# Cross-attention and ternary feed-forward on one core: the second normalisation's factors from one inverse root each, the output bias as a product of 128 rows, and new figures for the planner

## The chip, the cores and the metric

The kernel runs on one core of a Trainium2 chip. The core has a matrix engine (PE, TensorE; its weight loads are listed apart as PEld), a vector engine (DVE), a scalar engine (ACT), a general engine (POOL, GpSimd) and a queue engine (SP) that issues transfers; 16 DMA engines carry these out. The metric is device microseconds of one execution. The kernel before takes 1246.66 us (median of 3 runs, 1245.68 to 1249.71). A measurement of this kernel can tell a difference of about 0.3% from none.

## The reference

One decoder-like block on x of 4 x 2048 x 512 (float32), with a context of 4 x 77 x 512 and a mask over the 77 keys.

```python
def _layernorm(x, eps=1e-5):
    return (x - mean(x)) / sqrt(var(x) + eps)

# cross-attention, 16 heads of 32
Q = norm(x) @ Wq.T + bq;  K = ctx @ Wk.T + bk;  V = ctx @ Wv.T + bv
probs = softmax(where(mask == 0, -inf, Q K^T / sqrt(32)))
x = x + (probs V) @ Wo.T + bo

# feed-forward with quantised rows and ternary weights, hidden size 2048
act_quant(x):  s = 127 / clip(max|x| per row, 1e-5);  round(x * s) / s
weight_quant(w):  s = 1 / mean|w|;  clip(round(w * s), -1, 1) / s
h = act_quant(norm(x)) @ weight_quant(w1).T
h = silu(depthwise_conv1d(h, conv_w (3 taps), conv_b))     # along the sequence
x = x + act_quant(h) @ weight_quant(w2).T
```

A masked key takes the mean of the kept keys in the kernel and adds nothing to the sums. The quantity that the change is about is the second normalisation with the row's quantisation behind it: for each row of x after attention the mean, the variance, the largest |x - mean|, and from them the factor by which the row is multiplied before rounding and the factor that undoes it later (`dq`).

## The kernel before, in words

The 8192 rows are 64 blocks of 128 rows (`plan_block`, t = 0 to 63). Attention goes block by block; the query products go over pairs of blocks (`plan_queries`); the feed-forward goes over tiles of up to four blocks (`plan_hidden`, `TILES = [2, 2, 4, ..., 4, 3, 1]`, 18 tiles).

A block t passes these steps, each a `Step` with an engine, a cost in ns, a due time and the tiles that it uses and makes:

- First normalisation (`plan_norm`): ACT sums and squares (L714, L715), DVE scales the variance (L728), POOL takes the power -1/2 (L737) and applies it (L745). The result is split into two half-precision halves: the high half (`xn_hi`, ACT or POOL, L765 or L767, due at `O["hi"]`) and the low half (`xn_lo`, POOL, L795, due at `O["lo"]`). SP transposes both (`xn_transpose`, L800, due at `O["xT"]`).
- Query product of the pair on PE (L1067 to L1069, three products for the halves), bias on ACT or DVE (L1077, L1079).
- Scores in four groups of four heads on PE (L820), row maxima on DVE (L825), exponentials on ACT (L832). Due at `O["sc"]` and `O["sc_step"]` times the group.
- Probabilities in two halves of eight heads: split into high and low (L765 or L767, and L857 on POOL; due at `O["ph0"]`, `O["ph1"]`), transposed by SP (L861), multiplied by the values on PE (L869), divided by their sums on DVE (L881, L886).
- Context: split (L765 or L767, L918), transposed (L922), multiplied by the output weights on PE (`product`, L929 to L934). The first of its 13 matmuls, L929, is the output bias: three bfloat16 rows that add up to it (`bo3`, 3 x 512), multiplied by three rows of ones (`ones_bf`, 3 x 128).
- Residual on DVE (`residual`, L944): the product times a constant plus x, which SP has loaded a second time (`load_again`, L938, due at `O["xb"]` from the product), with the row's sum from the accumulator. L947 turns the sum into the negative mean. SP stores the block (L951) for the end.
- Second normalisation: `squares` on ACT (L970: (x - mean)^2 with their sum), `largest` on DVE (L977 the row's maximum of the squares, L978 variance plus eps), `roots` on POOL (L982: power 0.5 of the maximum and -0.5 of the variance in one operation), `scales` on DVE (L989 to L992, four operations on one number per row, each but one made from the one before), `quantise` on POOL (L997: add, multiply, to float16 with an offset of the exponent that rounds). SP transposes it (L1005); PE spreads `dq` over the columns (L689) and ACT copies it (L1013).

A tile of the feed-forward then goes through 16 groups of 128 hidden channels: product on PE (L1105), times `dq` on DVE (L1119), middle tap on ACT (L1130), the two other taps by the letter in `conv`: `b` both on DVE (L1145), `c` the first on DVE and the second on ACT and POOL (L1152, L1159), `d` both on ACT and POOL. Then SiLU on ACT (L1205), maxima on DVE (L1210), transposed maxima (L1241, L1246), scales on DVE (L1251 to L1256), spread and copied (L689, L1263), rounding on POOL (L1284), the second product on PE (L1304), the residual on DVE (L1314) and the store (L1320).

Which engine does a step that can go to two is set by `WHO`, one row for each stretch of blocks that `PARTS` bounds. Nothing at run time chooses: `Plan.schedule` walks through all steps in a modelled time, gives each engine the ready step with the earliest due time (in blocks, `t` plus an offset of the table `O`), takes the cost from the figure in `add`, and so writes one fixed order for each engine. The chip keeps that order and waits where a step's inputs or buffers are late. The buffers that bear on the change are `xb` (3), `xT` (2) and `qT` (8).

The two weights of the feed-forward are made ternary ahead (`plan_ternary`): `scale` (L644 to L649) takes the mean of |w|, from it the factor `deq` and its inverse.

Of the kernel before, what the change touches and what calls it, by code (L numbers as in the profile page):

```python
# [24 lines left out]
P = 128  # L25
# [52 lines left out]
PARTS = (12, 44, 56)  # L78
# [51 lines left out]
class Plan:  # L130
# [3 lines left out]

    LAT, SWITCH = {"PE": 197, "DVE": 130, "ACT": 130, "Pool": 75}, 1283
# [95 lines left out]
def xattn_bitffn_kernel(  # L231
# [123 lines left out]
    add("SP", 2500, -29, [], {"B": "y"}, load_ctx, lat=2300)  # L355
# [123 lines left out]
    add("DVE", 1700, -20, ["B"], {"kept": None}, kept_keys)  # L479
    for oc in range(EC):  # L480
# [4 lines left out]
            "DVE", 2000, pr, ["A", "B", ("kT", oc), "kept", ("s", "wq")], {("km", oc): None},  # L485
# [60 lines left out]
    for g in range(CG):  # L546
# [3 lines left out]
            "DVE", 1700, pr, [("pv", g), "kept"] + [("vm", g - 1)] * (g > 0),  # L550
# [37 lines left out]
    bo3 = fixed([3, E], BF16, "bo3")  # L588
# [15 lines left out]
    add("DVE", 3000, -11, [("s", "v"), ("s", "wo")], {"bos": None}, output_bias, lock=True)  # L604
    add("SP", 1800, -10, ["bos"], {"bo3": None}, gather_bias, lat=2300)
# [7 lines left out]
    def plan_ternary(dst, src, deq, name, prio):  # L613
# [28 lines left out]
        def scale():  # L642
# [20 lines left out]
        for i in range(2):  # L663
# [3 lines left out]
            for k in (2 * i, 2 * i + 1):  # L667
                eng = "ACT" if name in SUM_ACT else "DVE"
                add(eng, 2202, pr, [w], {(name, k, "t"): None}, partial(total, k))
        add(  # L670
            "DVE", 600, prio + 1.2, [(name, i, "t") for i in range(4)],
# [106 lines left out]
    def plan_block(t):  # L778
# [27 lines left out]
        add("SP", 400, early, [], {x: "x"}, load, lat=2500)  # L806
# [133 lines left out]
        def residual():  # L940
# [6 lines left out]
            nc.vector.tensor_scalar(o["rs"][:, 0:1], o["rs"][:, 0:1], -1.0 / E, None, ALU.mult)  # L947
# [15 lines left out]
        add("DVE", 800, t0 + 0.17, [xb, ("po", t), ("pod", t)], {("x1", t): None}, residual)  # L963
        add("SP", 350, t0 + 0.2, [xb, ("x1", t)], {("x1d", t): None}, keep, lat=2100)

        def squares():
# [4 lines left out]
                o["xm"], o["xb"], AF.Square, bias=r[:, 0:1], accum_out=r[:, 2:3]  # L971
            )

        def largest():

            r = o["rs"]
            nc.vector.tensor_reduce(r[:, 1:2], o["xm"], AX.X, ALU.max)  # L977
            nc.vector.tensor_scalar(r[:, 2:3], r[:, 2:3], 1.0 / E, EPS, ALU.mult, ALU.add)  # L978

        def roots():  # L980
            r = o["rs"][:, 1:3]
            nc.gpsimd.tensor_tensor(r, r, roots_of, ALU.pow)  # L982

        def scales():

            r = o["rs"]
            root, rstd = r[:, 1:2], r[:, 2:3]
            o["dq"] = small.tile([P, 1], F32, tag="dq1", name=f"dq_{t}")
            nc.vector.tensor_scalar(root, root, rstd, 1e-5, ALU.mult, ALU.max)  # L989
            nc.vector.tensor_scalar(o["dq"], root, deq1, None, ALU.mult)  # L990
# [411 lines left out]
```

## Time and profile before

| | us |
|---|---|
| median of 3 runs | 1246.66 (1245.68 to 1249.71) |
| the profiled execution, its own time | 1247.53 |
| its span, first to last instruction | 1245.7 |
| mean granted clock of TensorE | 0.968 |
| first bias product L929 starts / last | 97.8 / 1114.5 |
| first / last scales L989 | 115.6 / 1134.8 |
| TENSOR_REDUCE L977, mean | 0.671 |
| POOL power L982, mean | 0.707 |
| quantise L997, mean | 0.770 |

All times are of one execution. An engine's busy time is the union of its instructions. A row of the order of time gives the start, the duration, the engine, the line, and the operation with its operands; instructions of a pipelined engine overlap, so that the distance between starts, not the duration, is what one costs. In the list of waits the engine on the left stood idle until the instruction on the right was done; "issue" is idle time for which the profile shows no cause.

### The profile page before, as it was taken

What the parts mean: (1) busy time and instruction counts of PE and PEld (TensorE: products, weight loads), DVE (VectorE), ACT (ScalarE), POOL (GpSimd) and SP (SyncE); (2) the same over time, 40 slices, a digit from 0 to 9 for tenths busy, and PEclk for the clock granted to TensorE, in tenths of its full rate; (3) what the DMA queues carried; (4) which work ended last, traced back from release to release, by engine and by line L of the source; (5) the groups of instructions that cost most, each with busy time, mean ns of one, the idle gap of its engine ahead of it and who ended that gap; (6) DMA issues with size and microseconds to landing.
All of it is one profiled execution on the core that took longest, in us unless ns stands there. A gap on an engine that the chain in (4) does not pass through costs nothing. (4 is left out here: it accounts for less than half of the span.)

```text
span 1245.7 us, 24178 instructions
## 1 busy us (share of the span) xinstructions
PE 1122.5 (90%) x8191; PEld 732.2 (59%) x8191; DVE 1046.1 (84%) x2271; ACT 1016.0 (82%) x2345; POOL 982.8 (79%) x922
## 2 busy tenths in 40 slices
PE   4668889999899999999999999999999999986776
PEld 2345556666666666666666666666666665654332
DVE  5766488889899988988899989989998989998773
ACT  3666799989899888988989898989898988765651
POOL 3378767786897979697888879697979898778665
PEclk9869899999999999999999999999999999998987
DMA  7687967877676666667676767758576766541211
GB/s 246 250 183 158 186 126 137 175 172 151 133 154 160 140 156 155 157 149 168 136 161 144 190 145 165 154 145 179 132 166 163 166 127 160 121 111 47 68 60 58
DMA packets 403203, 185.45 MB, mean 149 GB/s; under 512 B 356307, under 2 KB 356947, under 8 KB 402568
## 3 DMA queue, kind: packets, MB, share of 16 engines
q1 hardware_dynamic: 402005, 183.62, 64.2%
q8 instruction: 64, 1.05, 0.4%
q14 instruction: 59, 0.48, 0.1%
q10 hardware_dynamic: 1075, 0.30, 0.1%
HBM read 65.13 MB, written 34.84 MB: 80 GB/s over the span
## 5 line engine op out<-in xcount | busy, mean ns | idle before, releaser
L1284 POOL TENSOR_TENSOR gq<-y,qsb 128x1024 f16<-128x1024 f32 (+3 forms) x144 | 309.6, 2167 | 11.9 <-PE pf L1304 10.6
L1105 PE MATMUL ph<-xqT,w1q 128*128 128x257 f16 (+3 forms) x2048 | 277.8, 277 | 18.1 <-DVE h L1119 17.3
L1304 PE MATMUL pf<-w2q,gq 128*128 128x512 fp8e4 x1024 | 265.7, 387 | 14.2 <-DVE xr L1314 7.7
L832 ACT ACTIVATE pr<-psc,nmx 128x77 f32<-128x77 f32 x1024 | 248.4, 337 | 27.7 <-DVE nmx L825 25.2
L1130 ACT ACTIVATE py<-h,cb_sb,cw_sb 128x512 f32<-128x512 f32 (+3 forms) x279 | 208.3, 747 | 68.2 <-DVE y L1145 67.8
L1105 PEld LDWEIGHTS <-w1q 128*128 128x128 fp8e4 x2048 | 198.5, 99 | 88.1 <-issue 38.4
L1119 DVE TENSOR_TENSOR h<-ph,dqb 128x514 f32<-128x514 f32 (+3 forms) x288 | 180.3, 626 | 39.9 <-PE ph L1105 37.8
L857 POOL TENSOR_TENSOR ph<-pr,ph 128x616 f16<-128x616 f32 x128 | 174.3, 1363 | 37.2 <-ACT ph L765 35.6
L820 PE MATMUL psc<-kblk,qT 128*128 128x308 f32 x512 | 184.1, 448 | 16.5 <-ACT pr L832 14.0
L1145 DVE SCALAR_TENSOR_TENSOR y<-h,cw_sb,py 128x512 f32<-128x512 f32 (+3 forms) x279 | 190.1, 681 | 10.4 <-POOL gq L1284 5.8
L1304 PEld LDWEIGHTS <-gq 128*128 128x128 f16 x1024 | 99.1, 99 | 108.8 <-issue 22.9
L1159 POOL TENSOR_TENSOR y<-y,ta 128x512 f32<-128x512 f32 (+3 forms) x100 | 114.2, 1142 | 54.9 <-ACT ta L1152 29.0
L1210 DVE TENSOR_REDUCE mx<-y 128x256 f32<-128x2048 f32 (+2 forms) x66 | 145.6, 2209 | 12.4 <-ACT y L1205 12.1
L1067 PE MATMUL pq<-xT,wq_hi 128*128 128x256 f16 x512 | 142.6, 279 | 12.8 <-DMA xT<-hl 6.4
L1069 PE MATMUL pq<-xT,wq_lo 128*128 128x256 f16 x512 | 142.5, 278 | 0.0
L1068 PE MATMUL pq<-xT,wq_hi 128*128 128x256 f16 x512 | 142.5, 278 | 0.0
L1145 DVE SCALAR_TENSOR_TENSOR py<-h,cw_sb,py 128x512 f32<-128x512 f32 (+3 forms) x197 | 135.7, 689 | 8.0 <-ACT py L1130 7.0
L825 DVE TENSOR_REDUCE nmx<-psc 128x4 f32<-128x308 f32 x256 | 118.5, 466 | 26.7 <-PE psc L820 26.1
L1205 ACT ACTIVATE y<-y 128x2048 f32<-128x2048 f32 (+3 forms) x72 | 120.1, 1712 | 1.6 <-POOL y L1159 1.2
L820 PEld LDWEIGHTS psc<-kblk,qT 128*128 128x128 f32 x512 | 87.7, 196 | 44.2 <-ACT pr L832 26.0
L869 PEld LDWEIGHTS <-prT 128*128 128x128 f16 (+1 forms) x1920 | 87.9, 98 | 43.6 <-DMA prT<-ph 24.2
L869 PE MATMUL pa<-vblk,prT 128*128 128x66 f16 (+2 forms) x1920 | 93.5, 201 | 18.2 <-DMA prT<-ph 12.6
(156 smaller groups left out, 2043.2 us busy)
## 6 DMA issues: line engine op xcount, KB each, us to landing
x<-in_x SPq DMA_DIRECT2D x64, 256.0 KB
xb<-in_x SPq DMA_DIRECT2D x64, 256.0 KB
x<-xb SPq DMA_DIRECT2D x64, 256.0 KB
xr<-x SPq DMA_DIRECT2D x64, 256.0 KB
out<-xr SPq DMA_DIRECT2D x64, 256.0 KB
w<-in_w1T SPq DMA_DIRECT2D x2, 2048.0 KB
w<-in_w2T SPq DMA_DIRECT2D x2, 2048.0 KB
prT<-ph SPq DMA_TRANSPOSE x128
```

The costliest lines, as they stand in the source:

```text
L820: nc.tensor.matmul(psc, pair[p]["q", c][:, half], kb[:, c], start=True, stop=True)
L832: nc.scalar.activation(o["pr", c // 2][:, n : n + NK], o["psc", c][:, h], AF.Exp, bias=o["nmx", c][:, h : h + 1],)
L857: nc.gpsimd.tensor_tensor(ph[:, 1, :HR], o["pr", hf], ph[:, 0, :HR], ALU.subtract)
L869: nc.tensor.matmul(pa[:, h0:h1], prT[:n, l + j], v[:, r], start=(j == 0 and i == 0), stop=(j == NS - 1 and i == 2), skip_group_check=True,)
L1067: nc.tensor.matmul(pq, hi[:, ic, os], xs[:, 0, ic], start=first, stop=False)
L1105: nc.tensor.matmul(ph[:, i, :WH], w1q[:, c, f * P : (f + 1) * P], xqT[:, c, c0 : c0 + WH], start=(c == 0), stop=(c == EC - 1),)
L1119: nc.vector.tensor_tensor(in_parts(s["h", f]), s["ph", f][:, :parts, :WH], in_parts(tile_a[a]["dqb"]), ALU.mult,)
L1130: nc.scalar.activation(dst, s["h", f][:, 1 : 1 + T], AF.Identity, bias=cb_sb[:, f : f + 1], scale=cw_sb[:, f, 1:2],)
L1145: nc.vector.scalar_tensor_tensor(ins[dst](), s["h", f][:, i : i + T], cw_sb[:, f, i : i + 1], ins[src](), ALU.mult, ALU.add,)
L1210: nc.vector.tensor_reduce(s["m", g][:, c0:c1], ys[g][:, :, c0:c1].rearrange("p c t i -> p t c i"), AX.XY, ALU.max, apply_absolute_value=True,)
L1284: engine.tensor_tensor(gq[u][:, :, :T], y, q, ALU.mult)
L1304: nc.tensor.matmul(s["po", k], gq[f // 2][:, f % 2, k * P : (k + 1) * P], w2q[:, f], start=(f == 0), stop=(f == HC - 1),)
```

## The change

- The residual keeps the plain row sum (L947 goes). `squares` takes 512 times the difference, (sum - 512 x)^2, by a factor in the activation; the constants behind it take the powers of 512 back.
- `largest` makes the variance first, then the maximum, then a third operation that raises the maximum to a floor that follows the variance.
- `roots` takes the power -0.5 of both numbers, into a tile of its own.
- `scales` makes three numbers with one operation each: a factor and an offset for `quantise` and `dq`. The factor of the first weight (`deq1`) is no longer in `dq`: it is multiplied into the tap weights `cw_sb` once, in `scale`. The dependency of `scales` on the mean of the first weight goes.
- `quantise` multiplies first and then adds.
- In the hidden tile's scales the multiplication L1254 goes; the copy on ACT becomes an activation with that factor.
- `ones_bf` is 128 x 128 and `bo3` 128 x 512, cleared, with the bias in its first three rows.
- The planner: new due times `O`, other engines for some steps (`WHO`, `PARTS`), new costs, and all PE costs times 1.04.

The diff, with what only changes a cost figure partly left out:

```diff
@@ -61,10 +61,10 @@
 O = {
-    "load": -4.06, "sa": -2.75, "na": -2.65, "hi": -4.58, "lo": -3.66, "xT": -2.53, "q": -1.68,
-    "q_step": 0.51, "sc": -0.43, "sc_step": 0.24, "ph0": 0.1, "ph1": 0.49, "v0": 0.1, "v1": -2.09,
-    "cx": 1.28, "o": 2.9, "n": 3.9, "xq": 3.51, "xb": -1.09, "h": 5.09, "s": 1.03, "p8": 0.63,
-    "p8_step": 0.33, "f": 2.33,
+    "load": -4.04, "sa": -2.75, "na": -2.68, "hi": -4.88, "lo": -2.65, "xT": -4.55, "q": -1.66,
+    "q_step": 0.51, "sc": -0.43, "sc_step": 0.0, "ph0": 0.09, "ph1": 1.04, "v0": 0.1, "v1": -2.17,
+    "cx": 1.28, "o": 2.94, "n": 3.71, "xq": 3.39, "xb": -1.77, "h": 5.09, "s": 1.03, "p8": 0.7,
+    "p8_step": 0.3, "f": 2.1,
 }
 SILU_ALL = False
 COUPLE = False
@@ -75,15 +75,15 @@
-PARTS = (12, 44, 56)
+PARTS = (12, 44, 54)
 WHO = [
     {"sa": "A", "sf": "D", "xh": "A", "ch": "A", "ph": "AA", "q": "AAAA",
      "conv": "ccbbbbbbbbbbbcbb", "round": "PPPPPPPP"},
     {"sa": "A", "sf": "D", "xh": "P", "ch": "A", "ph": "AA", "q": "AAAA",
      "conv": "cccbbbcbbbbbbcbb", "round": "PPPPPPPP"},
-    {"sa": "A", "sf": "D", "xh": "A", "ch": "P", "ph": "AA", "q": "DAAA",
-     "conv": "cccbbbcbbbbbbcbb", "round": "PPPPPPPP"},
-    {"sa": "A", "sf": "D", "xh": "A", "ch": "P", "ph": "AP", "q": "AAAA",
+    {"sa": "A", "sf": "D", "xh": "A", "ch": "P", "ph": "AA", "q": "AAAA",
+     "conv": "cccbcbcbbbbbccbb", "round": "PPPPPPPP"},
+    {"sa": "A", "sf": "D", "xh": "A", "ch": "A", "ph": "AP", "q": "AAAA",
      "conv": "dccbbdcbbbbbdccb", "round": "PPPPPPPP"},
 ]
@@ -132,12 +132,14 @@
...
+    PACE = {"PE": 1.04}
...
+        cost *= self.PACE.get(eng, 1.0)
...
@@ -282,10 +284,7 @@
...
-    roots_of = fixed([P, 2], F32, "roots_of")
-    nc.gpsimd.memset(roots_of[:, 0:1], 0.5)
-    nc.gpsimd.memset(roots_of[:, 1:2], -0.5)
-    ones_bf = fixed([3, P], BF16, "ones_bf")
+    ones_bf = fixed([P, P], BF16, "ones_bf")
...
@@ -476,13 +475,13 @@
...
-    add("DVE", 1700, -20, ["B"], {"kept": None}, kept_keys)
+    add("DVE", 1880, -20, ["B"], {"kept": None}, kept_keys)
...
-            "DVE", 2000, pr, ["A", "B", ("kT", oc), "kept", ("s", "wq")], {("km", oc): None},
+            "DVE", 2530, pr, ["A", "B", ("kT", oc), "kept", ("s", "wq")], {("km", oc): None},
...
@@ -585,7 +584,8 @@
...
-    bo3 = fixed([3, E], BF16, "bo3")
+    bo3 = fixed([P, E], BF16, "bo3")
+    nc.gpsimd.memset(bo3, 0.0)
...
@@ -601,8 +601,8 @@
...
-    add("DVE", 3000, -11, [("s", "v"), ("s", "wo")], {"bos": None}, output_bias, lock=True)
-    add("SP", 1800, -10, ["bos"], {"bo3": None}, gather_bias, lat=2300)
+    add("DVE", 4330, -11, [("s", "v"), ("s", "wo")], {"bos": None}, output_bias, lock=True)
+    add("SP", 2430, -10, ["bos"], {"bo3": None}, gather_bias, lat=2300)
...
@@ -645,8 +645,11 @@
             pt = new([P, E], F32, "m", f"pt_{name}")
             nc.tensor.matmul(pt[:, 0:1], ones, tot, start=True, stop=True)
             nc.vector.tensor_scalar(mean, pt[:, 0:1], 1.0 / (HID * E), 1e-5, ALU.mult, ALU.max)
-            nc.vector.tensor_scalar(deq, mean, 1.0 / 127.0, 1.0 / QUANTUM, ALU.mult, ALU.mult)
+            q = QUANTUM * E if name == "w1" else QUANTUM
+            nc.vector.tensor_scalar(deq, mean, 1.0 / 127.0, 1.0 / q, ALU.mult, ALU.mult)
             nc.vector.reciprocal(mean, mean)
+            if name == "w1":
+                nc.vector.tensor_scalar(cw_sb, cw_sb, deq, None, ALU.mult)
         def round_(i):
             st[name, "q", i] = new([P, 2, TMAX], I16, "gq", f"{name}_q{i}")
@@ -944,7 +947,6 @@
...
-            nc.vector.tensor_scalar(o["rs"][:, 0:1], o["rs"][:, 0:1], -1.0 / E, None, ALU.mult)
...
@@ -960,7 +962,7 @@
...
-        add("DVE", 800, t0 + 0.17, [xb, ("po", t), ("pod", t)], {("x1", t): None}, residual)
+        add("DVE", 752, t0 + 0.17, [xb, ("po", t), ("pod", t)], {("x1", t): None}, residual)
...
@@ -968,33 +970,39 @@
             r = o["rs"]
             o["xm"] = new([P, E], F32, "xm", name=f"xm_{t}")
             nc.scalar.activation(
-                o["xm"], o["xb"], AF.Square, bias=r[:, 0:1], accum_out=r[:, 2:3]
+                o["xm"], o["xb"], AF.Square, bias=r[:, 0:1], scale=-float(E),
+                accum_out=r[:, 2:3],
             )
         def largest():
             r = o["rs"]
-            nc.vector.tensor_reduce(r[:, 1:2], o["xm"], AX.X, ALU.max)
-            nc.vector.tensor_scalar(r[:, 2:3], r[:, 2:3], 1.0 / E, EPS, ALU.mult, ALU.add)
+            big, var = r[:, 1:2], r[:, 2:3]
+            nc.vector.tensor_scalar(var, var, 1.0 / E**3, EPS, ALU.mult, ALU.add)
+            nc.vector.tensor_reduce(big, o["xm"], AX.X, ALU.max)
+            nc.vector.tensor_scalar(big, var, 1e-10 * E**2, big, ALU.mult, ALU.max)
         def roots():
-            r = o["rs"][:, 1:3]
-            nc.gpsimd.tensor_tensor(r, r, roots_of, ALU.pow)
+            o["rt"] = small.tile([P, 2], F32, tag="rt", name=f"rt_{t}")
+            nc.gpsimd.tensor_tensor(o["rt"], o["rs"][:, 1:3], neg_half, ALU.pow)
         def scales():
-            r = o["rs"]
-            root, rstd = r[:, 1:2], r[:, 2:3]
+
+            total, big = o["rs"][:, 0:1], o["rs"][:, 1:2]
+            root, rstd = o["rt"][:, 0:1], o["rt"][:, 1:2]
+            o["f"] = small.tile([P, 2], F32, tag="fq", name=f"fq_{t}")
             o["dq"] = small.tile([P, 1], F32, tag="dq1", name=f"dq_{t}")
-            nc.vector.tensor_scalar(root, root, rstd, 1e-5, ALU.mult, ALU.max)
-            nc.vector.tensor_scalar(o["dq"], root, deq1, None, ALU.mult)
-            nc.vector.reciprocal(root, root)
-            nc.vector.tensor_scalar(rstd, rstd, root, 127.0 * QUANTUM, ALU.mult, ALU.mult)
+            nc.vector.tensor_scalar(o["f"][:, 0:1], root, 127.0 * QUANTUM * E, None, ALU.mult)
+            nc.vector.tensor_scalar(
+                o["f"][:, 1:2], total, root, -127.0 * QUANTUM, ALU.mult, ALU.mult
+            )
+            nc.vector.tensor_scalar(o["dq"], big, root, rstd, ALU.mult, ALU.mult)
         def quantise():
-            r = o["rs"]
+            f = o["f"]
             o["xq"] = new([P, E], F16, "xq", name=f"xq_{t}")
-            nc.gpsimd.tensor_scalar(o["xq"], o["xb"], r[:, 0:1], r[:, 2:3], ALU.add, ALU.mult)
+            nc.gpsimd.tensor_scalar(o["xq"], o["xb"], f[:, 0:1], f[:, 1:2], ALU.mult, ALU.add)
         def xq_transpose():
             if k == 0:
@@ -1030,9 +1038,9 @@
         sq, big, root, sc = (("xm", t), ("big", t), ("root", t), ("sc", t))
         x1 = [xb, ("x1", t)]
         add("ACT", 721, t0, x1, {sq: "xm"}, squares)
-        add("DVE", 660, t0 + 0.05, [*x1, sq], {big: None}, largest)
-        add("Pool", 545, t0 + 0.07, [big], {root: None}, roots)
-        add("DVE", 300, t0 + 0.1, [root, ("w1", "m")], {sc: None}, scales)
+        add("DVE", 930, t0 + 0.05, [*x1, sq], {big: None}, largest)
+        add("Pool", 670, t0 + 0.07, [big], {root: None}, roots)
+        add("DVE", 210, t0 + 0.1, [root], {sc: None}, scales)
         add("Pool", 735, t0 + 0.15, [*x1, sc], {xq: "xq"}, quantise)
         t0 = t + O["xq"]
         made = {("xqT", a): "xqT", ("dqb", a): "dqb"} if k == 0 else {}
@@ -1177,7 +1185,7 @@
...
-                        "Pool", 2.2 * T + 105, t0 + 0.22, [ta, y, y0 if i else py], {last: None},
+                        "Pool", 2.22 * T + 120, t0 + 0.22, [ta, y, y0 if i else py], {last: None},
...
@@ -1251,7 +1259,6 @@
...
-            nc.vector.tensor_scalar(s["qs"], s["qs"], 127.0, QUANTUM, ALU.mult, ALU.mult)
...
@@ -1260,7 +1267,9 @@
...
-            nc.scalar.copy(s["qsb"][:, :T], s["pb"])
+            nc.scalar.activation(
+                s["qsb"][:, :T], s["pb"], AF.Identity, scale=127.0 * QUANTUM
+            )
...
@@ -1289,7 +1298,7 @@
...
-            cost = dve(2 * T) if on_dve else 4.3 * T + 120
+            cost = dve(2 * T) if on_dve else 4.37 * T + 135
...

```

More of the change, by code (lines that the diff above doesn't have):

```diff
@@ L354, in xattn_bitffn_kernel @@
     add("SP", 2900, -30, [], {"A": "y"}, load_q, lat=2300)
-    add("SP", 2500, -29, [], {"B": "y"}, load_ctx, lat=2300)
+    add("SP", 920, -29, [], {"B": "y"}, load_ctx, lat=3500)
     add("SP", 2900, -28, ["B"], {"wk": None}, partial(load_square, "wk", wkT), lat=2300)
@@ L549, in xattn_bitffn_kernel @@
         add(
-            "DVE", 1700, pr, [("pv", g), "kept"] + [("vm", g - 1)] * (g > 0),
+            "DVE", 1925, pr, [("pv", g), "kept"] + [("vm", g - 1)] * (g > 0),
             {("vt", g): "h", ("vm", g): None}, partial(value_mask, g), lock=True,
@@ L668, in plan_ternary @@
                 eng = "ACT" if name in SUM_ACT else "DVE"
-                add(eng, 2202, pr, [w], {(name, k, "t"): None}, partial(total, k))
+                add(eng, 1890 if eng == "ACT" else 2195, pr, [w], {(name, k, "t"): None}, partial(total, k))
         add(
-            "DVE", 600, prio + 1.2, [(name, i, "t") for i in range(4)],
+            "DVE", 1200, prio + 1.2, [(name, i, "t") for i in range(4)],
             {(name, "m"): None, (name, "p"): "m"}, scale,
@@ L805, in plan_block @@
         early = -40 + t if t < 2 else t + O["load"]
-        add("SP", 400, early, [], {x: "x"}, load, lat=2500)
+        add("SP", 390, early, [], {x: "x"}, load, lat=2500)
         both = pair.setdefault(p, {})
@@ L1274, in plan_hidden @@
         uses = [("hm", a, g) for g in range(NG)] + [("w2", "m")]
-        add("DVE", 330, ts + 0.04, uses, {sc: None}, scales, lock=True)
+        add("DVE", 450, ts + 0.04, uses, {sc: None}, scales, lock=True)
         add("PE", 107 * n, ts + 0.08, [sc], {pb: "m"}, scale_transposes)
```

## The prediction

> **What bounds the kernel now.** I read the busy shares first, then the busy time of each engine by stage, then the waits of the middle stage, then the order of time on PE around the bias product and on DVE around the second normalisation.
>
> Busy shares over the whole span:
>
> ```profile
> PE 1122.5 (90%) x8191; PEld 732.2 (59%) x8191; DVE 1046.1 (84%) x2271; ACT 1016.0 (82%) x2345; POOL 982.8 (79%) x922
> ```
>
> By stage, the columns being start:end, length, then busy time (and instructions) of PE, PEld, DVE, ACT, POOL, then the granted clock, the DMA share and GB/s:
>
> ```profile
> 0.00:187.00 187.00, 132.79 (x849) 84.33 (x850) 120.81 (x303) 124.20 (x336) 112.74 (x128) 0.88 0.76 191
> 187.00:1090.00 903.00, 872.92 (x6725) 588.28 (x6724) 811.90 (x1759) 815.18 (x1894) 762.72 (x704) 1.00 0.70 154
> 1090.00:1245.70 155.70, 116.75 (x619) 59.63 (x617) 113.37 (x211) 76.59 (x116) 107.38 (x92) 0.90 0.23 69
> ```
>
> The reader is to see that 903 of 1245.7 us are one steady stage in which PE is busy 97% and the other three compute engines 84 to 90%. There PE sets the pace, and 30 us is all that it idles. The head has 54 us of PE idle and the end 39 us; both are latency, not load. Waits of the steady stage (waiting line, releaser, total us, times, longest):
>
> ```profile
> POOL rs L982 <- DVE rs L978: 33.6, 12, 5.4
> ...
> ACT xm L970 <- DVE rs L947: 16.6, 15, 2.8
> ...
> PEld L929 <- issue: 14.1, 44, 0.4
> ...
> PE pa L869 <- DMA prT<-ph: 8.0, 10, 2.4
> ```
>
> Two of them lie in the second normalisation, on engines with some idle time; the third is the weight load of the 3-row bias product, which nothing visible holds; the fourth is PE's longest own wait. On PE in order of time (start, duration):
>
> ```profile
> 606.12 1.05 PE L1105 MATMUL ph<-xqT,w1q 128*128 128x257 f16 x8
> 607.09 0.38 PE L929 MATMUL po<-bo,ones_bf 3*128 3x512 bf16 x1
> 607.41 0.39 PE L932 MATMUL po<-wo_hi,cT 128*128 128x512 f16 x1
> 607.64 0.38 PE L933 MATMUL po<-wo_lo,cT 128*128 128x512 f16 x1
> 607.85 0.38 PE L934 MATMUL po<-wo_hi,cT 128*128 128x512 f16 x1
> ```
>
> Matmuls of 512 columns start 0.215 us apart and overlap the one before by 0.17. The bias product overlaps its predecessor by only 0.08 (606.12 + 1.05 - 607.09), so it starts 0.09 late; the next one starts 0.32 after it, 0.105 late; the one after that 0.23, 0.01 late. That is 0.21 us for each block. The 64 places are nearly alike: medians 0.07, 0.32 and 0.23, which give the same 0.21. On DVE, in order of time:
>
> ```profile
> 600.74 0.14 DVE L978 TENSOR_SCALAR rs<-rs 128x1 f32<-128x1 f32 x1
> 600.80 0.14 DVE L728 TENSOR_SCALAR rs_xn<-rs_xn 128x1 f32<-128x1 f32 x1
> ...
> 604.08 0.20 DVE L989 TENSOR_SCALAR rs<-rs 128x1 f32<-128x1 f32 x1
> 604.31 0.21 DVE L990 TENSOR_SCALAR dq<-rs,scl 128x1 f32<-128x1 f32 x1
> 604.56 0.16 DVE L991 RECIPROCAL rs<-rs 128x1 f32<-128x1 f32 x1
> 604.76 0.21 DVE L992 TENSOR_SCALAR rs<-rs 128x1 f32<-128x1 f32 x1
> 604.89 0.68 DVE L1119 TENSOR_TENSOR h<-ph,dqb 128x514 f32<-128x514 f32 x1
> ...
> 613.56 0.08 DVE L944 DVE_READ_ACCUMULATOR xb<-po,inv_o,xb 128x1 f32 x1
> 613.67 0.15 DVE L947 TENSOR_SCALAR rs<-rs 128x1 f32<-128x1 f32 x1
> 613.74 0.47 DVE L825 TENSOR_REDUCE nmx<-psc 128x4 f32<-128x308 f32 x1
> ```
>
> A small operation that needs nothing of the one before lets the next start after 0.06 (L978) or 0.07 us (L947); one that the next depends on holds DVE for 0.20 to 0.25 us; the four of the scales take 0.81 in all.
>
> **The change part by part.**
>
> Bias product with 128 rows: same columns and passes, so its streaming time stays. Its weight load takes 91 ns now, the 128-row loads beside it 98, so loading more rows costs at most 0.01 us. What may go is the 0.21 us. From below, nothing goes if the loss belongs to the change of operand and not to the 3 rows; from above 0.21. L932, L933 and L934 also change weights and operands at every step and lose nothing, so I take 0.21. Seven of the 64 lie ahead of 187 us, where PE idles anyway; 57 x 0.21 = 12.0 us. The Trainium skill, TensorEngine Tiling (Array Packing), Key Properties, states that changing the tiling mode drains the TensorE; that is what a 3-row product between 128-row products would do, and by it the whole loss goes, 12 us, as by the rows.
>
> Residual: L947 goes. From the accumulator's read to the next operation it is 0.18 now and would be about 0.07: -0.11 us on DVE. The squares on ACT start that much sooner.
>
> Largest: the variance operation moves ahead of the reduction (same 0.06). A new operation with a pointer behind the reduction must see it finished: 0.12 (0.67 duration less the 0.59 after which L978 starts) plus 0.13 of its own, as L992: +0.25 us.
>
> Scales: three operations that need nothing of each other, 0.07 + 0.13 + 0.13 = 0.33 for 0.81: -0.48. Together -0.34 us of DVE for each block, 64 x 0.34 = 22 us off the path that PE sets. The skill's VectorE: DVE Perf Modes, Rules for kernel authors, speaks against this: chained operations aren't to be fused, since each drains anyway, and only their count matters. The count falls by one for each block (6 to 5), so by that rule about 13 us of DVE at 0.2 each go, not 22. Here the rows show starts 0.06 apart where nothing is needed, so the rows' value stands.
>
> What DVE's 22 us are worth: PE's waits that end on DVE in the steady stage are 3.5 us (h, L1119) and 1.4 us (cx, ahead of L929). Between 0 and these 4.9 us I take 2, as DVE's own load falls by only 2%.
>
> Roots: still one Pool power of 128x2 (706 ns), now into a tile of its own: 0. Quantise: same operation, multiply first: 0. Hidden scales: L1254 goes (169 ns median, 18 times), and the copy of the scales becomes an activation with a factor: between the copy's 585 ns and the 654 of L714, so 0 to +0.07 on ACT 18 times. Both lie beside PE's work: under 2 us in the last tiles' chain, taken as 0. The first mean now also multiplies the 128x48 tap weights: 0.23 (L418, 128x4) to 0.38 us (L472, 128x308) once at 59 us, beside the loads. Dropping the scales' dependency on that mean is worth 0: it is made at 58.6 us, the first scales run at 115.6 us. Clearing the 128x512 bias: about 0.46 us of Pool (vblk, 1584 columns in 1.41), before 9 us, where Pool idles 2.2 us; without that cover +0.46 once.
>
> Moves between engines: six query biases go from DVE (464 ns) to ACT (491): 3 us. Six second taps in the hidden tiles of blocks 44 to 55 go from DVE (0.74 each, 4.4 us) to ACT (0.71, 4.3 us) and Pool (1.14, 6.9 us). Ten context halves of blocks 54 to 63 go from Pool (0.62, 6.2 us) to ACT, two probability halves from ACT to Pool (1.4 us). Pool gets 2 us more in all, where it is busy 111.8 of 123 us (937 to 1060). Taken as 0: the next to be late there is the tap sum L1159, behind which the rounding L1284 queues.
>
> New order: due times shift, in blocks of 16.6 us (7.5 bias products in 125 us). The low half of the normalised rows (Pool, 1.16 us) comes 1.01 later; its transposition (SP, 1.27 us of issue) 2.02 earlier in rank, so it passes the prT, cT and xqT transpositions and the loads on SP whenever it is ready, and holds each by at most 1.27. The second probability half comes 0.55 later, with its Pool subtraction (1.36) and transposition; scores of one block fall due together, the last 0.72 earlier; the reload of x 0.64 earlier (0.57 us of SP), so its tile is held some 2.7 blocks of the 3 buffers instead of 2.2. The planner's figures come nearer to the trace: for the scales it charged 300 where 810 pass, for the residual 800 where 850 pass, for PE nothing of the 0.21. An order laid out with too short steps is where such waits as POOL rs on L978 (33.6 us) come from. The trace can't show the new order. Its gain ends at PE's 30 us of steady idle; its loss at the rival below, +32. I take -5, a sixth of that idle, nearer to nothing than to either end because PE's largest single wait, 8.0, is on prT, which the figures don't touch.
>
> Sum: -12.0 - 2 - 5 = -19. The profiled execution took 1247.53 (span 1245.7 and 1.8 around it), 0.9 above the median 1246.66. 1247.5 - 19 = 1228.5, less 0.9: about **1228 us**.
>
> **The rivals.**
>
> A. PE's gain comes, but 0.2 us earlier on PE only turns into waits for ACT, DVE and Pool, as they are at 84 to 90% and run in a fixed order. For it: ACT and DVE each have just 88 to 91 us idle out of 903, Pool waits 33.6 on one line. Against it: none of the large waits on PE is on DVE. 1242 to 1250 us.
>
> B. The order is much better than I take: most of the 30 us, say 22, goes with the 12: 1247 - 34 = about 1212, or a little below when the end shortens too. For it: the head and the end have 93 us of idle that other due times can reach. Against it: they are chains of latency.
>
> C. Slower: the normalised rows arrive late. For the second block of a pair the low half was due 0.98 block ahead of the query product (-2.66 to -1.68, in blocks from the pair's first); now they are due together (-1.65 and -1.66), and behind it come 1.16 us of Pool, 1.27 us of issue and the landing. If PE's order has the query product at its due place, PE stands still. The longest such wait now is 2.8 us, the sum 6.4 over 5. There are 32 pairs: from 14/32 = 0.44 us for each it eats the gain, at 1 us it is +32 and the time 1247 + 32 - 14 = 1265. Against it: the planner's own model carries that landing, and 8 query buffers leave over a block before the scores need them.
>
> D. The bias loss stays, as it isn't of the 3 rows: 1228 + 12 = 1240.
>
> **How the numbers follow.** Chances: my forecast 0.52 (1214 to 1238), B 0.15, D 0.06, A 0.10, C 0.17. What a measurement can tell from no change is about 0.3%, 3.7 us: 1242.9 to 1250.4. Faster: 0.52 + 0.15 + 0.06 and 0.03 of A: 0.76; same: the rest of A, 0.07; slower: C, 0.17. The range from 1206 to 1250 leaves out most of C and the lower end of B, under 2 in 10.
>
> **What would show it.** Bias product: 128*128 in its row, the next start 0.215 us after it, no "issue" wait of L929 and L932. DVE: L947's line gone, three small rows within 0.4 us, and after the reduction one row that starts 0.7 us after it. Order: PE's idle time in the steady stage under 30 us; in C, PE's wait for xT far above 6.4 us. The prediction is wrong if the bias product keeps its 0.32, if PE's idle grows by what the product gave, or if head or end lengthen.

## The result, and the profile after

The changed kernel is slower: 1258.32 us median (1255.37 to 1264.05) beside 1249.31 us of the kernel before (1245.68 to 1250.07), six runs each, the three named ahead among those of the kernel before. The ratio is 1.0082, 95% interval 1.0057 to 1.0107. The forecast was 1228 with a range of 1206 to 1250. The profiled execution took 1258.08 us, its span is 1256.2.

The page of the kernel after, busy shares, and then its stages (start:end, length, busy time and instructions of PE, PEld, DVE, ACT, POOL, clock, DMA share, GB/s), at the cuts that the prediction used:

```profile
PE 1116.4 (89%) x8191; PEld 734.8 (58%) x8191; DVE 1029.6 (82%) x2178; ACT 1023.8 (81%) x2365; POOL 983.2 (78%) x919
```

```profile
0.00:187.00 187.00, 128.87 (x817) 83.28 (x818) 123.21 (x293) 124.02 (x338) 110.35 (x125) 0.86 0.76 192
187.00:1090.00 903.00, 860.84 (x6698) 586.14 (x6698) 787.87 (x1667) 817.96 (x1901) 755.36 (x698) 1.00 0.71 152
1090.00:1256.20 166.20, 126.68 (x678) 65.39 (x676) 118.48 (x219) 81.83 (x129) 117.45 (x98) 0.91 0.26 72
```

In the steady stage PE is busy 12 us less than before, and yet fewer instructions pass in the same 903 us: 6698 matmuls instead of 6725. Those 27 matmuls, at 0.13 us of busy time each, account for some 3.5 of the 12 us; the rest is what the arithmetic took from PE, and it is there as idle time: 42 us, 30 before.

The two places that the prediction costed, in the order of time, first PE around the bias product (L932 is now its line), then DVE in the second normalisation (L947 residual, L981 to L983 `largest`, L996 to L1000 `scales`):

```profile
610.34 0.27 PE L1077 MATMUL pq<-xT,wq_lo 128*128 128x256 f16 x1
610.45 0.38 PE L932 MATMUL po<-bo,ones_bf 128*128 128x512 bf16 x1
610.67 0.38 PE L935 MATMUL po<-wo_hi,cT 128*128 128x512 f16 x1
```

```profile
601.81 0.14 DVE L981 TENSOR_SCALAR rs<-rs 128x1 f32<-128x1 f32 x1
601.87 0.67 DVE L982 TENSOR_REDUCE rs<-xm 128x1 f32<-128x512 f32 x1
602.58 0.21 DVE L983 TENSOR_SCALAR rs<-rs 128x1 f32<-128x1 f32 x1
...
605.93 0.14 DVE L996 TENSOR_SCALAR fq<-rt 128x1 f32<-128x1 f32 x1
605.99 0.20 DVE L997 TENSOR_SCALAR fq<-rs,rt 128x1 f32<-128x1 f32 x1
606.11 0.27 DVE L1000 TENSOR_SCALAR dq<-rs,rt 128x1 f32<-128x1 f32 x1
606.29 0.47 DVE L828 TENSOR_REDUCE nmx<-psc 128x4 f32<-128x308 f32 x1
...
615.08 0.08 DVE L947 DVE_READ_ACCUMULATOR xb<-po,inv_o,xb 128x1 f32 x1
615.08 0.47 DVE L828 TENSOR_REDUCE nmx<-psc 128x4 f32<-128x308 f32 x1
```

Both work as costed. The matmul behind the bias product starts 0.22 us after it (0.32 before). The "issue" wait of the bias product's weight load (L929 before, 14.1 us) is gone, and that of the load behind it fell from 12.4 us (L932 before) to 3.9 (L935). The scales take 0.36 us up to the next start (0.81 before, 0.33 forecast), the new operation starts 0.71 us after the reduction, and the next work starts at once behind the accumulator's read. So the loss lies elsewhere. Waits of the steady stage after the change (waiting line, releaser, total us, times, longest):

```profile
PE pa L872 <- DMA prT<-ph: 24.6, 31, 2.1
...
POOL xq L1005 <- DVE fq L997: 15.6, 15, 3.7
...
POOL rt L987 <- DVE rs L983: 15.4, 11, 4.9
...
PE pq L1075 <- DMA xT<-hl: 2.3, 3, 1.0
```

PE's wait for the transposed probabilities grew from 8.0 to 24.6 us. POOL's wait in the second normalisation, which the prediction put down to too short steps in the plan, fell from 33.6 (L982) to 15.4 us (L987). The wait for xT, which the prediction's rival C names, is 2.3 in this stage (2.1 before). But the 6.4 us by which the prediction would judge rival C were of the whole span, and there it is 14.5 now. It grew in the first 187 us, here before and after:

```profile
PE pq L1067 <- DMA xT<-hl: 4.3, 2, 2.8
```

```profile
PE pq L1075 <- DMA xT<-hl: 12.2, 2, 8.5
```

Which of this is cause, the experiments ask.

### The profile page after: what moved, and what is told of

Its sections match the earlier page's. It is cut to its first block, busy times and chain, and to the rows that moved or that the text cites. A ratio compares the mean times of both kernels' runs of the same rounds, so it can differ in the third digit from the quotient of the medians.

```text
span 1256.2 us, 24138 instructions
## 1 busy us (share of the span) xinstructions
PE 1116.4 (89%) x8191; PEld 734.8 (58%) x8191; DVE 1029.6 (82%) x2178; ACT 1023.8 (81%) x2365; POOL 983.2 (78%) x919
## 5 line engine op out<-in xcount | busy, mean ns | idle before, releaser
L1127 DVE TENSOR_TENSOR h<-ph,dqb 128x514 f32<-128x514 f32 (+3 forms) x288 | 180.8, 628 | 35.9 <-PE ph L1113 33.6
L1167 POOL TENSOR_TENSOR y<-y,ta 128x512 f32<-128x512 f32 (+3 forms) x106 | 121.8, 1149 | 74.7 <-DVE y L1153 33.6
L1075 PE MATMUL pq<-xT,wq_hi 128*128 128x256 f16 x512 | 142.7, 279 | 18.5 <-DMA xT<-hl 14.5
L1218 DVE TENSOR_REDUCE mx<-y 128x256 f32<-128x2048 f32 (+2 forms) x66 | 145.7, 2211 | 12.6 <-ACT y L1213 12.4
L1153 DVE SCALAR_TENSOR_TENSOR py<-h,cw_sb,py 128x512 f32<-128x512 f32 (+3 forms) x191 | 131.3, 688 | 17.5 <-ACT py L1138 17.1
```

Source lines behind the costliest of these rows:

```text
L1075: nc.tensor.matmul(pq, hi[:, ic, os], xs[:, 0, ic], start=first, stop=False)
L1127: nc.vector.tensor_tensor(in_parts(s["h", f]), s["ph", f][:, :parts, :WH], in_parts(tile_a[a]["dqb"]), ALU.mult,)
L1153: nc.vector.scalar_tensor_tensor(ins[dst](), s["h", f][:, i : i + T], cw_sb[:, f, i : i + 1], ins[src](), ALU.mult, ALU.add,)
L1218: nc.vector.tensor_reduce(s["m", g][:, c0:c1], ys[g][:, :, c0:c1].rearrange("p c t i -> p t c i"), AX.XY, ALU.max, apply_absolute_value=True,)
```

## The experiments

All ratios are against the kernel before, timed on the same chip. The groups of runs were on different chips, so ratios are compared, and a difference in us is that of two ratios times 1249. Since every engine's order is written out by the planner, one can change the arithmetic and keep the order, or the reverse.

### The arithmetic and the order apart

`code_only` takes every edit of the arithmetic and no figure, due time or engine; the dependency of the scales on the first weight's mean stays in the plan, so that each engine has the order of before. `plan_only` is the reverse: the arithmetic of before in the new order. `bias_only` and `norm_only` split `code_only`.

```diff
 code_only: before.py with
-    ones_bf = fixed([3, P], BF16, "ones_bf")        # and bo3, likewise
+    ones_bf = fixed([P, P], BF16, "ones_bf")
     residual, squares, largest, roots, scales, quantise, hidden scales as in the change
     O, WHO, PARTS, PACE and all costs as before
 plan_only: before.py with O, WHO, PARTS, PACE and the costs of the change
 bias_only: before.py with ones_bf and bo3 alone
 norm_only: code_only without ones_bf and bo3
```

> The arithmetic of the change (second normalisation, 128-row bias, hidden scales) with the planner's figures, due times and engines of before, so that every engine keeps the order of before. Theory 1 (the new order loses, the arithmetic gains): PE's 12 us show, about 1237 against 1249 (ratio 0.990); PE's wait for transposed probabilities stays at the 8 us that it had in the steady stage. Theory 2 (what PE saves turns into waits for the other engines whatever the order): 1246 to 1252 (ratio 0.998 to 1.002) and PE's idle time in the steady stage grows by 8 to 12 us.

> The arithmetic of before with the new figures, due times and engines, so that every engine has the order of the changed kernel. Theory 1: the order alone loses what the arithmetic gains and 9 us more, about 1270 (ratio 1.017), with PE waiting 20 us or more for transposed probabilities in the steady stage. Theory 2: the order is worth nearly nothing by itself: 1250 to 1259 (ratio 1.000 to 1.008).

> Only the output bias as a product of 128 rows, everything else and the order as before. By the rows on PE 0.21 us go at each of 64 places: the next matmul 0.215 us after the bias product instead of 0.32, and 1249 - 12 = about 1237 (ratio 0.990). If PE's gain becomes waits elsewhere: 1247 to 1250 with the same 0.215.

> Only the second normalisation and the hidden scales in their new form, bias product of 3 rows, order as before. Off PE's path: 1246 to 1249 (ratio 0.998 to 1.000), DVE busy about 20 us less. If the new operation behind the maximum delays POOL's power and with it the chain to the first feed-forward product, 1250 to 1255.

| | median us | ratio | 95% interval |
|---|---|---|---|
| code_only | 1233.33 | 0.9874 | 0.9833 to 0.9914 |
| plan_only | 1271.15 | 1.0178 | 1.0147 to 1.0208 |
| bias_only | 1247.45 | 0.9982 | 0.9965 to 0.9998 |
| norm_only | 1239.37 | 0.9914 | 0.9882 to 0.9945 |

Theory 1 holds. The arithmetic alone gains 1.26%, 15.7 us of 1249; the order alone loses 1.78%, 22 us. Their product, 0.9874 x 1.0178 = 1.0050, lies a little under the 1.0082 of the change. `code_only` beats both kernels. PE's wait for the transposed probabilities in the steady stage is 11.2 us in `code_only`, where theory 1 had it stay at 8, and 20.7 in `plan_only`.

Inside the arithmetic the split was not as forecast. The bias product alone gave 2 us where 12 were forecast; that is the second case of its expectation, in which PE's gain becomes waits. The normalisation gave 10.7 where 2 were forecast, more than either case of its expectation. In `bias_only` the mechanism is complete, as its order of time on PE shows:

```profile
608.64 0.38 PE L930 MATMUL po<-bo,ones_bf 128*128 128x512 bf16 x1
608.86 0.38 PE L933 MATMUL po<-wo_hi,cT 128*128 128x512 f16 x1
```

but its steady stage shows PE busy 5.7 us less than before and no more matmuls through (6729, 6725 before):

```profile
187.00:1090.00 903.00, 867.26 (x6729) 591.87 (x6733) 812.62 (x1762) 816.80 (x1897) 764.95 (x705) 1.00 0.70 154
```

`norm_only`, on the other hand, leaves PE's instructions as they are and moves the 903 us on by 45 matmuls; DVE's busy time over the whole span is 1026.7 us, 19.4 less than before:

```profile
187.00:1090.00 903.00, 875.15 (x6770) 591.93 (x6769) 803.09 (x1706) 816.78 (x1899) 769.85 (x709) 1.00 0.70 155
```

So a PE that is busy 97% was not the only thing that set the pace. Over the whole span the two runs differ in where the time went: `bias_only` has PE 8.5 us less busy and 8.3 us more idle than before, `norm_only` has PE idle as long as before (123.4 and 123.2 us) and 7.1 us less busy with the same 8191 matmuls. How shorter work on DVE shortens PE's busy time no run shows.

Where the order loses is seen when the span is cut at the first and the last bias product. `code_only` first, then the kernel after, each with the stretch from first to last bias product:

```profile
97.90:1099.50 1001.60, 952.78 (x7438) 652.36 (x7445) 872.99 (x1893) 898.84 (x2118) 847.73 (x798) 0.99 0.71 156
```

```profile
102.30:1127.70 1025.40, 963.89 (x7461) 652.58 (x7459) 877.71 (x1885) 910.33 (x2144) 852.84 (x797) 1.00 0.71 153
```

With nearly the same numbers of matmuls in each part, 23.8 of the 27.4 us by which the spans differ (1228.8 and 1256.2) lie in this stretch, 4.4 in the head before it, and the end gains 0.8. Not all of it is idle time of PE: over the whole span PE idles 15.7 us longer and is busy 11.7 us longer (1104.7 and 1116.4; the trace of `code_only` lacks 8 of the 8191 matmuls).

### Due times or figures, and the wait for the transposed probabilities

```diff
 after_old_due: after.py with O of before
 code_new_due:  code_only with O of the change
 after_no_pace: after.py with
-    PACE = {"PE": 1.04}
+    PACE = {}
 after_landing: after.py with the landing of each kind of transposition 1250 ns longer in the plan
-                lat=2450,       # prT; xT and cT 2250, xqT 1550
+                lat=3700,       # prT; xT and cT 3500, xqT 2800
```

> The changed kernel with the due times of before; new cost figures, PE costs times 1.04 and new engines stay. The order was shown to lose about 22 us; this asks which half of it does. Theory D (the new due times lose): close to the arithmetic alone, 1232 to 1242. Theory F (the new figures lose, above all the factor on PE, which takes away the lead that PE's costs had left to the transposed probabilities): 1250 to 1262, with PE waiting over 15 us for them in the steady stage.

> The new arithmetic with the old figures and the old engines, but the new due times. Theory D: 1252 to 1262, PE waits over 15 us for transposed probabilities. Theory F: 1230 to 1240 and at most 11 us of that wait, as with the arithmetic alone.

> The changed kernel without the factor 1.04 on PE's costs, everything else of it kept. Theory F: half or more of the loss comes back, 1238 to 1248. Theory D: 1254 to 1264.

> The changed kernel with 1250 ns more for the landing of each of the four kinds of transposition in the planner's figures (the arithmetic and everything else unchanged), because PE's waits in the trace end 4.3 to 5.2 us after the issue, where the planner counts 3.8. Theory L (PE is sent to the products of the values too early, because the landing is charged too low): the wait falls from 25 us to under 10 in the steady stage and the time to 1238 to 1250. If the landing isn't it: 1253 or more.

| | median us | ratio | 95% interval |
|---|---|---|---|
| after_old_due | 1271.11 | 1.0185 | 1.0156 to 1.0214 |
| code_new_due | 1260.93 | 1.0098 | 1.0077 to 1.0118 |
| after_no_pace | 1259.54 | 1.0084 | 1.0065 to 1.0103 |
| after_landing | 1259.45 | 1.0082 | 1.0060 to 1.0105 |

Neither theory D nor theory F holds alone. With the new arithmetic, new due times on old figures lose 28 us against `code_only`, old due times on new figures and engines lose 39, and both new together 26. Only the old pair is fast: the old due times are slow with the new figures, and the new due times are as slow with the old figures as with the new ones (the intervals of 1.0098 and 1.0082 overlap). The factor on PE explains nothing: without it the time is the same.

The time does not follow the wait for the transposed probabilities either. In the steady stage PE waits for them 24.6 us in the kernel after, 16.8 in `after_no_pace`, 16.0 in `code_new_due`, which are all about as slow, and 16.2 in `after_old_due`, which is the slowest. `after_landing` takes the wait away, as its waits of the steady stage show:

```profile
PEld L872 <- DMA prT<-ph: 6.8, 12, 1.4
PE pa L872 <- DMA prT<-ph: 2.3, 3, 0.9
```

and the time stays at 1.0082. PE's busy time over the span is 1117.8 us of 1254.3, so its idle time is 136.5, where the kernel after has 139.8 and `code_only` 124.1. In the steady stage something did come back. `code_only` first, then `after_landing`:

```profile
187.00:1090.00 903.00, 869.28 (x6782) 595.68 (x6787) 806.94 (x1713) 817.36 (x1899) 775.22 (x715) 1.00 0.70 155
```

```profile
187.00:1090.00 903.00, 869.82 (x6747) 596.28 (x6759) 795.47 (x1688) 822.87 (x1917) 764.99 (x703) 1.00 0.71 153
```

With 6747 matmuls it stands between the 6698 of the kernel after and the 6782 of `code_only`. Yet what was left then, 48 matmuls fewer than in the kernel after (630 and 678; its trace lacks 14 of the 8191), took 164.3 us where that took 166.2. The longer landings give every engine another order, so what the wait costs by itself stays open. Shown is that taking it away is not enough.

### Is the old order special?

```diff
 near_q:  code_only with    -"q": -1.68   +"q": -1.63
 near_cx: code_only with    -"cx": 1.28   +"cx": 1.33
 near_p8: code_only with    -"p8": 0.63   +"p8": 0.68
 after_near_xq: after.py with -"xq": 3.39 +"xq": 3.44
```

> The new arithmetic, old figures and engines, old due times but for one: the query product due 0.05 of a block later (-1.63 for -1.68), which gives each engine another order without any of the new figures. Theory S (the order of before is by itself unusually good on the chip, and nearly any other order of the same steps costs 15 us or more): 1248 to 1262. Theory P (the loss belongs to what is new, the due times and the figures): near the arithmetic alone, 1231 to 1243.

> As the run before, but the one due time is that of the context's split, 1.33 for 1.28; the order of PE is the old one up to its 477th of 1312 steps. Theory S: 1242 to 1258, part of the loss as part of the order. Theory P: 1231 to 1243.

> As the two before, but the one due time is that of the rounding, 0.68 for 0.63. Theory S: 1248 to 1262. Theory P: 1231 to 1243.

> The changed kernel with one due time moved, the transposition of the quantised rows 3.44 for 3.39. Theory S: an ordinary neighbour of an ordinary order, within 8 us of the changed kernel, 1250 to 1266. If the order of the changed kernel were itself a good pick among its neighbours: 1268 or more.

| | median us | ratio | 95% interval |
|---|---|---|---|
| near_q | 1240.33 | 0.9923 | 0.9888 to 0.9959 |
| near_cx | 1246.21 | 0.9969 | 0.9953 to 0.9986 |
| near_p8 | 1242.33 | 0.9933 | 0.9911 to 0.9954 |
| after_near_xq | 1259.54 | 1.0088 | 1.0058 to 1.0117 |

Both theories have a part. One due time moved by a twentieth of a block (0.8 us) gives a ratio 0.5 to 0.95% above that of `code_only`, 6 to 12 us. The interval of `near_cx` is clear of that of `code_only`; those of the two others overlap it, and all three lie on one side. No figure of the planner differs in them. So part of the old order's speed seems not to survive such shifts; clear of noise that is for `near_cx` alone. A neighbour of the changed kernel, by contrast, is as slow as that kernel. The mean of the three, 0.9942, leaves 1.0082 - 0.9942 = 1.4%, some 17 us, for what is new; that a small shift is the right measure of what any other order costs is argued, not shown. How the old due times were found is not on record either: had they been picked among measured neighbours, most shifts would lose against them, and no run here can tell.

### Which group of the new

```diff
 due_norm: code_only with the new load, na, hi, lo, xT
 due_prob: code_only with the new sc_step, ph0, ph1, v1
 due_late: code_only with the new o, n, xq, xb, p8, p8_step, f, q
 code_who: code_only with the new PARTS and WHO
```

> New arithmetic, old figures and engines, and of the new due times only those of the first normalisation: load, application, high half, low half and the transposition xT. If the prediction's rival C holds (the normalised rows come late), 1250 to 1265 and PE waits over 10 us for xT; if this group is an ordinary shift, 1237 to 1247 as with single due times moved by 0.05.

> As the run before, but only the new due times of the scores and of the probabilities' halves (sc_step, ph0, ph1, v1). If the second half's split, due 0.55 of a block later, makes PE wait for the transposed probabilities, 1250 to 1262 and over 25 us of that wait; if ordinary, 1237 to 1247.

> As before, but only the new due times behind attention: output product, reload of x, second normalisation, its transposition, rounding, second product, and the query product's. If this group carries the loss, 1250 to 1262, with the wait on DVE or POOL rather than on transposed probabilities; if ordinary, 1237 to 1247.

> New arithmetic, old figures and old due times, the new engines (query biases, taps, context halves). The moves are worth 2 us of POOL in all: an ordinary shift of the order, 1237 to 1247; if POOL is overloaded by the six taps between 890 and 1090 us, 1248 or more with the loss in that stretch.

| | median us | ratio | 95% interval |
|---|---|---|---|
| due_norm | 1239.45 | 0.9928 | 0.9900 to 0.9956 |
| due_prob | 1238.93 | 0.9939 | 0.9922 to 0.9956 |
| due_late | 1245.84 | 0.9997 | 0.9978 to 1.0017 |
| code_who | 1244.30 | 0.9974 | 0.9955 to 0.9992 |

No group carries the loss: all four lie within what a shift of 0.05 costs or, for `due_late`, a little above. Against `code_only` the three groups of due times lose 0.5, 0.65 and 1.2%; together that is 2.4%, and all of them at once (`code_new_due`) lost 2.2%. So the loss seems to add up from many places; the sum is rough, since the interval of `code_only`, 0.4% to each side, enters it three times. The due times of rival C do not carry the loss: with them the rows' split and xT's rank move as in the change and cost what any shift costs, and PE's wait for xT in the steady stage of `due_norm` is (line, releaser, total us, times, longest)

```profile
PE pq L1073 <- DMA xT<-hl: 1.2, 2, 1.0
```

In its first 187 us that wait is 3.0 us. The 12.2 of the changed kernel come with the whole new plan: `plan_only`, with the old arithmetic, has 12.5 there, and `after_old_due`, with the new figures and the old due times, 8.5.

The new engines, 2 us more on POOL by the count of the prediction, cost 1.0%, 12 us: not nothing, but not above a shift either.

### What a third of a microsecond on one engine is worth

```diff
 code_only with a spare 128x256 tile, written once for each block and used by nothing
 dummy_dve, at the end of scales:
+            nc.vector.tensor_tensor(spare, twice, twice, ALU.mult)
 dummy_act, at the end of dq_copy:
+            nc.scalar.copy(spare, twice)
```

`twice` is the identity matrix read two times over.

> The new arithmetic in the order of before, plus one operation for each block that nothing uses: a 128x256 product on DVE behind the three scales (0.42 us long, 0.34 to the next start, as the context's 128x256 row), off the normalisation's chain. Theory E (the time of the engine counts): the 10 us that the second normalisation gained come back, 1240 to 1248 beside 1249 before. Theory K (the shorter chain gained it): 1231 to 1238.

> The same with a 128x256 copy on ACT behind the spread of the factor. ACT has as much idle time in the steady stage as DVE. Theory E for every engine: 1240 to 1248; if DVE alone sets the pace: 1231 to 1238.

`dummy_dve`: 1261.36 us, ratio 1.0099 (1.0069 to 1.0130). `dummy_act`: 1238.48 us, ratio 0.9910 (0.9882 to 0.9937). The copy on ACT takes its 0.41 us (median 408 ns), adds 15.9 us to ACT's busy time, and the time grows by 0.36%, 4.5 us, which the intervals don't part from nothing. `dummy_dve` lies above both of its forecasts. The operation on DVE cost far more than intended, because it was not 0.42 us long. DVE and POOL of `dummy_dve`, in order of time:

```profile
605.80 0.27 DVE L1000 TENSOR_SCALAR dq<-rs,rt 128x1 f32<-128x1 f32 x1
605.94 4.95 POOL L1294 TENSOR_TENSOR gq<-y,qsb 128x1024 f16<-128x1024 f32 x2
605.99 2.63 DVE L1001 TENSOR_TENSOR spare<-ident 128x256 f32<-128x256 f32 x1
608.54 0.68 DVE L1128 TENSOR_TENSOR h<-ph,dqb 128x514 f32<-128x514 f32 x1
```

It ends about when the first of POOL's two roundings (2.4 us each) does; over the 64 places it took 0.41 to 2.63 us, 0.88 in the median. The busy share on the page is

```profile
PE 1110.9 (89%) x8182; PEld 734.3 (59%) x8191; DVE 1083.3 (86%) x2254; ACT 1015.5 (81%) x2345; POOL 995.8 (79%) x921
```

that is 56.9 us more DVE than in `code_only` (1026.4), for a time 28 us longer: half a microsecond for each microsecond of DVE. But the operation did not stay off the normalisation's chain. `quantise` on POOL is the step behind the scales; in `code_only` and in `dummy_dve` (busy us, mean ns | idle time before it) it took

```profile
L1003 POOL TENSOR_SCALAR xq<-xb,fq 128x512 f16<-128x512 f32 x64 | 49.9, 780 | 6.6 <-DVE fq L995 5.8 <-DMA x<-in_x 0.8
```

```profile
L1006 POOL TENSOR_SCALAR xq<-xb,fq 128x512 f16<-128x512 f32 x64 | 58.9, 920 | 8.6 <-DVE fq L997 8.4
```

At 49 of the 64 places it overlaps the spare product and takes 0.97 us in the mean, at the others 0.76 to 0.78. So the run made DVE busier and the chain longer at once, and does not tell theory E from theory K. `norm_only` gained 10.7 us for 19.4 us less DVE, a rate of 0.55, and it too shortened the chain. That DVE's time counts at about half is therefore an estimate that both runs fit, with the chain's part in it not shown. For ACT the rate is 0.28, and the intervals leave room from nothing to about two thirds, so that ACT is not shown to differ from DVE.

## Why the prediction was wrong, point by point

- **Bias product.** The loss of 0.21 us at each place, its cause in the 3 rows, and its going were right; rival D falls. The step that failed is the term "57 x 0.21 = 12.0 us", which took PE's time at full worth because PE was busy 97%. Alone it is worth 2.2 us (0.0018, interval 0.0002 to 0.0035); added to the normalisation (0.9914 to 0.9874) it is worth 5, though these two intervals overlap. Rival A had that right for this term: PE's gain turned into waits, 8.5 us less busy and 8.3 more idle in `bias_only`.
- **Second normalisation.** The rows were right: 0.36 us for the scales (0.33 forecast), 0.71 behind the reduction, 19.4 us less DVE in all (22 forecast, over the 64 blocks, the hidden scales beside it). The rule of the Trainium skill's VectorE: DVE Perf Modes, Rules for kernel authors, to keep down the count of operations, gave 13 when taken alone; the rows of the scales disagree with that, as one operation fewer saved 0.45 us and not 0.2. What failed is "Between 0 and these 4.9 us I take 2". The list of PE's waits has five more rows that name DVE, 3.6 us together, so that the bound was 8.5 by its own reasoning. And those waits are not all that DVE's time costs: it was worth 10.7 us, with PE's idle time unchanged. Whether the shorter chain or DVE's freed time gained it is open.
- The two errors cancel, by luck: 14 us were forecast for the arithmetic, 15.7 measured.
- **New order.** This is the step that made the forecast wrong: "-5, a sixth of that idle". The order costs +22 with the old arithmetic and +26 with the new. The argument that figures nearer to the trace give a better order had no run behind it; `after_old_due` and `code_new_due` show the opposite for due times that were made for other figures, and the new pair is still slower than the old one. The wait that the argument named, POOL's on L978, did shrink, from 33.6 to 15.4 us (34.7 in `code_only`, with the old order), and the time grew all the same; PE's wait on prT, "which the figures don't touch", grew from 8.0 to 24.6. The bound of +32 for the order was wide enough, but its chance, 0.17, hung on one mechanism (rival C), which occurred only in the head: of the 8.1 us by which PE's wait for xT grew, 7.9 lie in the first 187 us. Two of the prediction's signs of being wrong came true: PE's steady idle time grew by 12 us, and the head lengthened.
- **Head and end.** The head is 4.5 us longer to the first bias product (97.8 to 102.3), the end 2.7 us shorter. In the head PE waits 7.9 us longer for xT, but no run shows the cause of its lengthening. With the old figures and the new due times the first bias product began at 101.9, with single groups of due times at 98.7 to 99.6; in `bias_only`, with the order of before, it began at 100.4, so that part of such differences is not of the order.
- **Engines moved.** Taken as 0, measured 12 us against `code_only`, within what any shift of the order costs.

What stays open is why the old pair of figures and due times suits the chip better by some 1.4% than the new one beyond what any small shift costs. The runs exclude, as the one cause, PE's factor and any single group of due times, the rows' transposition with them; they speak against the wait for the transposed probabilities, without giving its own price.

## What to carry to other kernels

Where an order is written out ahead for four engines that are all 84 to 97% busy, measure the arithmetic in the old order before the plan is made anew: here that alone was 1.3% faster, and the new plan cost more than it had gained. Don't read the busiest engine's busy share as the rate at which its time counts: here a microsecond of the 12 on PE was worth 0.2 to 0.4 (2.2 us alone, 5 beside the normalisation), one of the 19.4 on DVE 0.55 (10.7). And a wait that grows is not yet the cause: take it away, see whether the time goes with it, and look at what else the same edit moved, in the order and on other engines.

## What the runs showed of the hardware that was not expected

- A DVE product whose two inputs both lie in SBUF, while POOL works on SBUF, took 0.41 to 2.63 us for the same 128x256 elements. The Trainium skill, SBUF — State Buffer, Who interferes with whom, states that a DVE instruction with two SBUF inputs contends with a GpSimd instruction that reads SBUF, and that the port pair they share is an exclusive lock; the row above, 2.63 us under a rounding of POOL, agrees. The products that the kernel runs next to it (h, with one input from PSUM) kept their 0.68 us. POOL pays as well: `quantise` took 0.97 us where it overlapped this product, 0.76 to 0.78 where it did not.
- A due time moved by 0.05 of a block, 0.8 us, put three neighbours of the old order 6 to 12 us behind it, one of them clear of the interval; the same shift left the changed kernel within 1 us (1.0088 and 1.0082). So such a shift can be as large as the single edit that one would want to judge by it.
